# Moving the exponentials' quarters per head group, with ScalarE copying the own quarters, in a two-layer graph kernel with a hand-written order

## The chip, the core and the metric

The kernel runs on one core of a Trainium2 chip. The metric is device time in microseconds (us) of one execution. TensorE (PE in the profile, its weight loads PEld), VectorE (DVE), ScalarE (ACT) and GpSimd (POOL) compute; SyncE (SP) issues nearly all DMAs, and its queue is SPq in the profile.

## The reference

Two layers over 128 graphs of 128 nodes with 256 features, all in float32. Cut to what matters:

```python
# layer 0: attention with an adjacency mask, then an FFN
q, k = heads(src @ Wq + bq), heads(src @ Wk + bk)          # 8 heads of 32
attn = softmax(q k^T / sqrt(32), axis=-1)                  # over all nodes
out = sum over r in 0..3 of (attn * (adj == r)) @ heads(src @ Wv[r] + bv[r])
x = ln(src + out @ Wo + bo); x = ln(x + gelu(x @ W1 + b1) @ W2 + b2)
# layer 1: two graph attentions, then an FFN
for W, a in (W1, a1), (W2, a2):
    Wh = h @ W
    e = leaky_relu(Wh @ a[:256] + (Wh @ a[256:])^T, 0.2)
    h = softmax(where(adj > 0, e, -9e15), axis=1) @ Wh
x = ln(x + h); x = ln(x + relu(x @ w_ff1 + b) @ w_ff2 + b)
```

The adjacency holds only 0 and 1. The softmax's sums in layer 0 run over all nodes, so they need the exponentials before the mask.

## The kernel before

The 16384 rows are worked in 32 groups (NG) of 512 rows: 4 graphs. A group has two pairs p of graphs. For each group there are generators, one for each kind of work, which issue a few instructions per step: `in` and `rest` load; `bo` prepares the residual; `q` makes q, k and v (tiles pqqa, pqqb, pvqa, pvqb on TensorE; `projected`, from group 2 on with seven products in place of eight); `a` is attention; `d` gathers the softmax's sums; `n0` to `n3` are the layer norms, which also copy x into 16-bit planes (L464) and transpose them by DMA into pT (L467); `t0` to `t2` copy pT into yT (L492); `f` and `fc` are two halves of the first FFN, `l` the two graph attentions (pw L1093, py, pg on TensorE), `k` and `kc` the second FFN, `out` the store.

The order in which all these steps are issued is written by hand in three strings, FRONT, STEADY and TAIL. A token is a step and the group it is for, relative to the current one; `a:1*3` takes three steps of the next group's attention. STEADY is run for groups 1 to 29. Nothing reorders it: each engine runs its instructions in the order of these tokens, and waits on semaphores where data or a buffer isn't ready.

The FFNs multiply with seven products of half-size blocks. `others` works in the banks ph1/po1 (tag fa) and ph7/po7 (tag fe), `chain` in the one bank seeded: ScalarE copies the first product into seeded (L620, L647, L649), TensorE adds products to it, ScalarE copies it out (p16 L628, and p7 L583 from ph7), VectorE forms hT's quarters (L591 from ph7, L632 from seeded) and their sums h2, h3 (L640 to L644). A product that reuses seeded waits for its last reader.

In attention, `scores` makes four tiles ps, one for each head group s (L858), and one exponential for each (L865) into e, a tile of 128 partitions with the keys along the partitions: `e[:, s]` is 512 numbers for each key. `masked` multiplies by the adjacency into pm (L875); `sums` multiplies e and pm with v into pav (L970). e, pm and es have one buffer each.

The softmax's sums are taken on VectorE from group 2 on (`turned_sums`). Key quarters (32 partitions each) and head groups must be exchanged so that four quarters of a head group lie on the same partitions. For that SP moves 32-partition blocks of e into four parts: es[:, 0], es[:, 1], and ea's two; for p=0 ea lies in the upper half of pm, for p=1 in the tag wh. Then VectorE adds the four (L901, L903, L905), transposes and reduces. Part k of head group s comes from quarter (s + k) mod 4, so that part 0 is a copy within the same partitions. pm's upper half is masked only when the sums over it are folded.

Of the kernel before, what the change touches and what calls it, by code (L numbers as in the profile page):

```python
# [120 lines left out]


FRONT = """
in:0 Lqk*4 Lgat q:0 Lv Lo q:0*2 wqk q:0 rest:0 q:0 L1 Lv*3 q:0*3 a:0 Lv_ a:0 Lv_ q:0 a:0*2 in:1
Lv_ d:0 a:0*2 d:0*2 q:0 a:0 d:0*4 q:0 a:0 L3 d:0 a:0 q:0 L1 q:0 L1 q:0 a:0 Lh1 a:0*6 Lh1 a:0 L2
L1 a:0*2 d:0 a:0 q:1 L1 d:0 Lg1 a:0*2 L4 d:0 q:1*2 q:0 w1 d:0*3 a:0 rest:0 q:1 w1 q:1 d:0 q:1*2
d:0 q:0 a:0 q:1 a:0*2 a:1*3 Lg1 bo:0*2 L1 a:0*2 wqk Lgat rest:1 a:1*2 Lg1 a:1 a:0*2 L2 d:1*2 a:0
L2 d:1 L4 Lg1 a:1 a:0 L3 a:0*4 d:1 bo:0 b1 q:1 d:1 n0:0 d:1 a:1 d:1 rest:1 q:1 n0:0 b1 q:1 d:1
n0:0 q:1*2 output_bias n0:0 a:1 n0:0 w1 n0:0 output_bias Lh1 q:1 b1 wv a:1*2 w1 a:1 gw n0:0 t0:0
a:1*2 t0:0 a:1 f:0 t0:0*2 a:1 b1 a:1*2 L3 d:1 t0:0 fc:0 a:1 b1 t0:0 a:1 d:1 L2 q:1 a:1 d:1*2 Lgat  # L130
Lg2 f:0 q:1 fc:0 wqk Lgat fc:0 b1 f:0 L4 a:1 d:1 Lg2 a:1 b1 fc:0 d:1 f:0 L3 d:1 Lh1 d:1 b1 f:0
a:1 f:0 a:1 w2 Lh2 fc:0 f:0 fc:0 a:1 fc:0 w2 f:0 fc:0 gw fc:0 L4 gw f:0 a:1*2 fc:0 wv a:1*2
bo:1*2 fc:0 wv in:2 L3 fc:0 L3 f:0 fc:0*2 f:0 wqk a:1 f:0 a:1 fc:0 f:0 fc:0 f:0*2 a:1*2 fc:0*2 w2
f:0 c1 fc:0*3 rest:2 fc:0 a:1*2 f:0 fc:0 w2 f:0 n0:1 c1 fc:0 n0:1*2 fc:0 n0:1*2 f:0*2 fc:0 q:2
f:0*2 n0:1 bo:1 fc:0*3 n0:1 f:0 q:2 fc:0 f:0 t0:1 fc:0 t0:1 fc:0 gw n1:0*2 q:2 t0:1*2 gw gelu
n1:0 q:2 n1:0 q:2 n1:0 c1 q:2 f:1 q:2 n1:0 t0:1 c1 q:2*2 n1:0 q:2 t1:0 c1 t1:0 f:1 q:2 l:0 fc:1
t0:1 f:1 t1:0 l:0 u1 l:0 t1:0 fc:1 l:0*4 f:1 fc:1 l:0 fc:1 f:1 Lh2 q:2 l:0 f:1 fc:1 q:2*2 fc:1*2
f:1 fc:1 f:1 fc:1 q:2 fc:1 q:2*2 f:1 fc:1 q:2 u2 l:0 c1 l:0*2 f:1 c1 fc:1 l:0 a:2 l:0*2 f:1 a:2
f:1 l:0 a:2 fc:1 l:0*2 a:2 exp l:0*2 q:2 a:2 u2 l:0*4 fc:1 wv l:0*3 q:2 u2 fc:1*2 q:2 d:2 l:0
fc:1 d:2 f:1 l:0 fc:1 q:2 u1 fc:1 u1 f:1*2 d:2 f:1 q:2 u1 d:2 q:2 d:2 q:2 l:0 a:2*2 fc:1 l:0*2  # L140
f:1 fc:1 q:2 d:2 q:2 fc:1 l:0 c1 l:0*2 f:1 q:2 f:1 l:0*2 fc:1 l:0*2 fc:1 l:0*2 u2 d:2 l:0 fc:1
l:0*2 f:1 fc:1 l:0*2 n2:0 f:1 d:2 n2:0*6 t2:0 fc:1 t2:0 fc:1 q:2 t2:0 fc:1 a:2*2 rest:2
"""
STEADY = """
q:1 f:0 q:1*2 f:0 t2:-1 fc:0 a:1*4 k:-1 fc:0 d:1 f:0 a:1*2 t2:-1 d:1 kc:-1 t2:-1 a:1*3 k:-1*2
fc:0 d:1 kc:-1 a:1 kc:-1 a:1 k:-1 a:1 k:-1 a:1*3 d:1*2 n1:0 k:-1 kc:-1 d:1 k:-1 kc:-1 k:-1 n1:0
k:-1 kc:-1 n1:0 a:1 kc:-1 n1:0*2 a:1 kc:-1 bo:1 n1:0 d:1 a:1 k:-1 kc:-1 d:1*3 a:1*5 kc:-1*4 k:-1
n1:0 in:2 kc:-1 t1:0*2 k:-1*2 t1:0 k:-1 kc:-1 t1:0 k:-1 l:0*2 k:-1 kc:-1 k:-1 bo:1 l:0*2 kc:-1
bo:1 a:1*2 kc:-1 l:0 kc:-1 a:1 l:0 kc:-1 l:0 a:1 l:0*2 k:-1 n0:1 kc:-1*2 n0:1 kc:-1 k:-1 kc:-1
k:-1 n0:1 kc:-1 n0:1*2 k:-1 kc:-1*2 n0:1 rest:2 n0:1 l:0*2 kc:-1 l:0*2 kc:-1 k:-1 l:0 q:2 t0:1  # L150
q:2 t0:1 q:2 l:0*2 k:-1 t0:1 kc:-1 l:0 f:1 l:0*2 t0:1 kc:-1 q:2*2 fc:1 q:2 t0:1 q:2 f:1*2 l:0
t0:1 q:2 gelu f:1 l:0*3 k:-1 l:0 fc:1 q:2 kc:-1 l:0 fc:1 l:0 fc:1*2 l:0 f:1*2 q:2 l:0 fc:1*2 l:0
f:1 fc:1 f:1 fc:1 n3:-1 f:1 fc:1*2 f:1 fc:1 q:2 fc:1 f:1 q:2 n3:-1 f:1*3 fc:1 l:0 q:2 fc:1 l:0
f:1 q:2 fc:1 q:2 l:0 n3:-1 q:2 f:1 l:0 q:2 fc:1*2 q:2 f:1 fc:1 l:0*2 fc:1 a:2 fc:1 f:1 fc:1 a:2
l:0 a:2 l:0*4 f:1 a:2 q:2 a:2 fc:1 a:2 l:0 a:2 l:0*2 q:2 l:0 q:2 l:0 d:2*2 fc:1 f:1 q:2*2 l:0
d:2*2 q:2 d:2 q:2 n2:0 d:2 out:-1 fc:1 n2:0 f:1 n2:0 fc:1 n2:0*4 q:2 t2:0*3 d:2 fc:1 q:2 fc:1 q:2
fc:1 q:2 d:2 a:2 exp rest:2 a:2
"""
TAIL = """
q:1 f:0 t2:-1 q:1*2 d:1 fc:0*2 a:1 t2:-1 f:0 a:1*3 f:0 a:1 fc:0 k:-1 a:1 k:-1 kc:-1 a:1 k:-1*2  # L160
d:1 k:-1 a:1 t2:-1 d:1 kc:-1 k:-1 n1:0 a:1 kc:-1 n1:0 kc:-1 k:-1 a:1 kc:-1 d:1 n1:0 d:1 k:-1 a:1
n1:0 kc:-1 k:-1 n1:0 a:1*3 kc:-1 a:1 bo:1 kc:-1*3 k:-1 kc:-1 d:1 kc:-1 k:-1 d:1 n1:0 k:-1 kc:-1
a:1 k:-1 n1:0 t1:0 d:1 t1:0 kc:-1 a:1*2 l:0 d:1*2 kc:-1 l:0 t1:0 a:1 kc:-1 l:0 bo:1 t1:0 k:-1 a:1
l:0*5 a:1 k:-1 a:1 l:0 a:1*4 k:-1 kc:-1 a:1 k:-1 kc:-1 bo:1 kc:-1*2 k:-1 n0:1 kc:-1*2 n0:1
kc:-1*2 k:-1 kc:-1 l:0*3 k:-1 kc:-1 l:0 n0:1 l:0 n0:1 l:0 n0:1*3 t0:1 l:0*2 t0:1 l:0*2 k:-1*2 l:0
kc:-1 l:0 kc:-1*2 l:0*2 kc:-1*2 t0:1 l:0*3 k:-1 t0:1 kc:-1 l:0*2 t0:1 f:1 fc:1 l:0 f:1 l:0*4 t0:1
f:1 fc:1 l:0 fc:1 l:0*2 f:1 l:0 f:1 fc:1*2 f:1 fc:1 f:1 fc:1 l:0*2 f:1*3 l:0 fc:1*2 l:0 fc:1*4
k:-1 f:1 fc:1 f:1 fc:1 l:0*2 f:1 fc:1 f:1*2 l:0 f:1 fc:1*2 l:0*2 fc:1 n2:0 f:1 fc:1 gelu n3:-1
fc:1*2 f:1 fc:1 n2:0 fc:1 n2:0 f:1 n2:0 fc:1 n2:0 f:1 fc:1 n3:-1 fc:1 n2:0 fc:1 f:1 n2:0 t2:0 f:1
fc:1 f:1*2 exp fc:1*2 t2:0 k:0 fc:1 t2:0 n1:1 t2:0 kc:0 t2:0 n1:1*2 t2:0 k:0 kc:0 n1:1 k:0*2 n1:1  # L170
kc:0 n1:1*2 k:0 kc:0*2 t1:1*2 kc:0 n3:-1 k:0*2 kc:0 out:-1 l:1*3 t1:1*2 l:1*3 k:0 l:1*2 kc:0*2
l:1*3 kc:0*2 l:1 k:0 l:1 kc:0 l:1*3 k:0 l:1 k:0 l:1 k:0 l:1 kc:0 k:0*2 kc:0 l:1*5 k:0 l:1*9 k:0
kc:0*2 l:1*2 kc:0*3 k:0 kc:0 l:1*5 kc:0*2 l:1*6 kc:0*2 n2:1 kc:0 k:0 n2:1*4 kc:0 k:0 kc:0 k:0*2
n2:1*2 kc:0 t2:1 k:0 t2:1 kc:0 k:0 t2:1 kc:0*2 k:1 t2:1 kc:1 t2:1 k:1 t2:1 kc:1*2 checks k:1*2
kc:1 k:1*2 kc:1 k:1 kc:1 k:1 kc:1*2 k:0 k:1 kc:0 kc:1*4 k:1 kc:1 k:1*2 kc:1 n3:0 k:1*2 kc:1 k:1*2
kc:1 k:1 kc:1*6 n3:0 k:1 kc:1*2 k:1*2 n3:0 kc:1*2 k:1*2 kc:1*3 k:1*2 z:1 kc:1 z:1 kc:1*2 out:0
z:1*2
"""


# [8 lines left out]
def fast_pass(ctx, tc, a, out):  # L189
# [651 lines left out]
    def scores(S, p):  # L841

        assert {(0, 0, p), (0, 1, p)} <= S["have"]
        qT, kT = S["qT"], S["kT"]
# [17 lines left out]
        yield 1 if p == 0 else None
        S["e", p] = e = w1p.tile([P, HC, 2, NCH, P], F32, tag="e", name="e_" + n)
        for s in range(HC):
            nc.scalar.activation(e[:, s], pss[s], AF.Exp, scale=SCALE)  # L865
# [15 lines left out]
    def turned_sums(S):  # L881

        n = str(S["g"])
        for p in range(G // 2):
            e = S["e", p]
            es = w1p.tile([P, 2, T], F32, tag="es", name=f"es_{n}_{p}")
            ea = None
            if p:
                ea = flat(w1p.tile([P, G, NU], F32, tag="wh", name="ea_" + n))
                ea = ea[:, : 2 * T].rearrange("p (k t) -> p k t", k=2)  # L890
            for k in range(4):
                if k == 2 and p == 0:
                    ea = S["pm", p][:, 2:].rearrange("p s u c i -> p s (u c i)")
                part = (es, ea)[k // 2][:, k % 2]
                for s in range(HC):
                    to, fr = (slice(y * DH, (y + 1) * DH) for y in (s, (s + k) % HC))
                    nc.sync.dma_start(part[to], e[fr, s].rearrange("p u c i -> p (u c i)"))  # L897
# [5 lines left out]
            nc.vector.tensor_add(ea[:, 0], ea[:, 0], ea[:, 1])  # L903
# [679 lines left out]
```

## Time and profile before

| | |
|---|---|
| median of 3 runs | 2649.66 us (2648.33 to 2652.46) |
| the profiled execution: time, span | 2651.96 us, 2650.1 us |
| granted TensorE clock, mean | 0.997 |
| PE busy, 20362 matmuls | 2597.7 us, 98% |
| DVE busy, 6041 instructions | 2324.8 us, 88% |
| ACT busy, 3599 instructions | 1715.9 us, 65% |
| queue of SP and ACT (q1): share of 16 DMA engines | 33.2% |
| L897, the moves of e | 960 issues of 64 KB |
| L875, masking | 162.9 us, 256 instructions of 686 ns mean |
| L865, exponentials | 136.4 us, 256 instructions of 603 ns mean |

Busy times of engines lie beside each other; they don't add up to the span. A matmul's end is modelled, so distances between the starts of matmuls tell more than busy time. In a timeline row the columns are the start in us from the span's start, the length in us, the engine, the line, the operation, output and inputs, and in brackets how long the engine stood idle and what ended that.

### The profile page before, as it was taken

What the parts mean: (1) busy time and instruction counts of PE and PEld (TensorE: products, weight loads), DVE (VectorE), ACT (ScalarE), POOL (GpSimd) and SP (SyncE); (2) the same over time, 40 slices, a digit from 0 to 9 for tenths busy, and PEclk for the clock granted to TensorE, in tenths of its full rate; (3) what the DMA queues carried; (4) which work ended last, traced back from release to release, by engine and by line L of the source; (5) the groups of instructions that cost most, each with busy time, mean ns of one, the idle gap of its engine ahead of it and who ended that gap; (6) DMA issues with size and microseconds to landing.
All of it is one profiled execution on the core that took longest, in us unless ns stands there. A gap on an engine that the chain in (4) does not pass through costs nothing.

```text
span 2650.1 us, 54615 instructions
## 1 busy us (share of the span) xinstructions
PE 2597.7 (98%) x20362; PEld 2293.6 (87%) x20362; DVE 2324.8 (88%) x6041; ACT 1715.9 (65%) x3599; POOL 154.2 (6%) x137
## 2 busy tenths in 40 slices
...
DMA packets 328896, 202.11 MB, mean 76 GB/s; under 512 B 234288, under 2 KB 276400, under 8 KB 328624
## 3 DMA queue, kind: packets, MB, share of 16 engines
q1 hardware_dynamic: 327520, 198.16, 33.2%
q8 instruction: 162, 2.65, 0.4%
...
## 4 chain that ended last, share of the span: by engine, by line
PE 68%; DVE 14%; DMA 7%; ACT 6%; SPq 4%; issue 2%; DVEq 0%; POOL 0%; ACTq 0%; POOLq 0%
PE po L533 12%; PE ph L524 12%; PE seeded L524 10%; PE seeded L533 8%; PE pw L1093 4%; PE pqqa L788 4%; SPq L897 3%; PE pav L970 3%; PE pqqb L788 3%; DMA pT<-planes 3%; PE pwo L1016 2%; PE ps L858 2%; PE py L1106 2%; PE pvqa L788 2%; DMA spread<-hbm 1%
## 5 line engine op out<-in xcount | busy, mean ns | idle before, releaser
L492 ACT COPY yT<-pT 128x512 uint16<-128x512 uint16 x384 | 266.7, 763 | 146.0 <-DMA pT<-planes 145.7
L464 ACT COPY planes<-x 128x512 uint16<-128x512 uint16 x384 | 222.8, 619 | 157.7 <-DVE x L444 155.8
L430 POOL TENSOR_TENSOR rs<-rs,mhalf 128x4 f32<-128x4 f32 x129 | 152.0, 1179 | 2441.5 <-DVE rs L429 2423.2
L524 PE MATMUL seeded<-yS,w_L_gnn_w_ff 128*128 128x256 f32 x768 | 204.5, 389 | 10.0 <-ACT seeded L620 7.9
L865 ACT ACTIVATE e<-ps 128x512 f32<-128x512 f32 x256 | 136.4, 603 | 107.0 <-issue 73.8
L524 PE MATMUL seeded<-yS,w_L_gnn_W 128*128 128x256 f32 x768 | 198.0, 380 | 0.3 <-DVE yS L504 0.3
L524 PE MATMUL ph<-yT,w_L_gnn_W 128*128 128x256 f32 x768 | 193.1, 380 | 0.5 <-ACT yT L492 0.4
L524 PE MATMUL ph<-yT,w_L_gnn_w_ff 128*128 128x256 f32 x768 | 191.0, 384 | 1.3 <-ACT seeded L647 0.7
L406 DVE BATCH_NORM_STATS2 st<-x 128x6 f32<-128x256 f32 x512 | 189.3, 412 | 1.5
L533 PE MATMUL po<-w_L_gnn_w_ff,hT 128*128 128x128 f32 x1536 | 189.7, 277 | 0.0
L533 PEld LDWEIGHTS po<-w_L_gnn_w_ff,hT 128*128 128x128 f32 x1536 | 179.5, 192 | 10.7 <-ACT hT L548 10.4
L533 PE MATMUL po<-w_L_gnn_W,hT 128*128 128x128 f32 x1536 | 187.1, 275 | 0.0
L533 PEld LDWEIGHTS po<-w_L_gnn_W,hT 128*128 128x128 f32 x1536 | 184.0, 192 | 3.2
L548 ACT ACTIVATE hT<-hT,c_L_gnn_b_ff 128x256 f32<-128x256 f32 x256 | 113.1, 502 | 112.2 <-DVE hT L591 111.4
L524 PEld LDWEIGHTS seeded<-yS,w_L_gnn_w_ff 128*128 128x128 f32 x768 | 139.5, 190 | 47.9 <-ACT seeded L620 19.5
L875 DVE TENSOR_TENSOR pm<-e,adj 128x512 f32<-128x512 f32 x256 | 162.9, 686 | 4.0 <-ACT e L865 2.9
L805 ACT COPY pv<-pvqa 128x512 f32<-128x512 f32 x60 | 35.2, 587 | 201.7 <-PE pvqa L788 201.5
L524 PEld LDWEIGHTS seeded<-yS,w_L_gnn_W 128*128 128x128 f32 x768 | 144.2, 190 | 23.6 <-ACT p L628 0.7
L524 PEld LDWEIGHTS ph<-yT,w_L_gnn_w_ff 128*128 128x128 f32 x768 | 143.0, 190 | 24.3 <-ACT seeded L647 1.5
L524 PEld LDWEIGHTS ph<-yT,w_L_gnn_W 128*128 128x128 f32 x768 | 143.3, 190 | 19.4 <-ACT yT L492 1.0
L1093 PE MATMUL pw<-wu,yT 128*128 128x260 f32 x512 | 139.6, 398 | 8.6 <-ACT yT L492 7.5
L632 DVE TENSOR_TENSOR hT<-seeded,p 128x512 f32<-128x512 f32 x128 | 88.1, 688 | 62.0 <-PE seeded L524 60.2
...
## 6 DMA issues: line engine op xcount, KB each, us to landing
es<-e SPq DMA_DIRECT2D x480, 64.0 KB, 2.0
...
pm<-e SPq DMA_DIRECT2D x240, 64.0 KB, 2.0
ea<-e SPq DMA_DIRECT2D x240, 64.0 KB, 2.0
...
```

The costliest lines, as they stand in the source:

```text
L406: nc.vector.bn_stats(st[:, b % 2, :], S["x"][:, b, :])
L430: nc.gpsimd.tensor_tensor(rs[:, bs], rs[:, bs], k.mhalf[:, bs], op=ALU.pow)
L464: nc.scalar.copy(planes[:, :, b], words)
L492: nc.scalar.copy(o.rearrange("p (b t h) -> p h b t", b=2, h=2), pT[:, :, :, c, :])
L524: nc.tensor.matmul(bank[:, s * TH : (s + 1) * TH], wa[:, form, 0, f * P : (f + 1) * P], m, start=start and s == 0, stop=True, skip_group_c ...
L533: nc.tensor.matmul(bank[:, s * P : (s + 1) * P], m[:, f, s * P : (s + 1) * P], wb_[:, form, f, :], start=start and s + f == 0, stop=True, ...
L548: nc.scalar.activation(o[:, s], o[:, s] if src is None else src[:, s * TH : (s + 1) * TH], func, bias=ba[:, f : f + 1],)
L632: nc.vector.tensor_add(hidden(1, 1, r), halves(seeded), halves(B["7", r]))
L788: nc.tensor.matmul(bank[:, s * TH : (s + 1) * TH], *ops, start=start and s == 0, stop=True, skip_group_check=True,)
L865: nc.scalar.activation(e[:, s], pss[s], AF.Exp, scale=SCALE)
L875: nc.vector.tensor_mul(pm[:, s], S["e", p][:, s], S["ad"][:, pair(p), None, :].to_broadcast([P, 2, NCH, P]),)
L1093: nc.tensor.matmul(pw[:, :NU], yT[:, c, b * P : (b + 1) * P], wu[:, c, :], start=(c == 0), stop=(c == NCH - 1),)
```

## The change

In `turned_sums`, the loop over parts with the head groups inside becomes a loop over head groups with three moves each (parts 1 to 3), in one step per head group. Part 0, the own quarter, is no longer moved but copied by ScalarE, four copies of 32x512 in two steps. For groups from 2 on, pm of p=0 is allocated behind the first exponential and not the last. FRONT, STEADY and TAIL are replaced whole. The core of the diff:

```diff
 STEADY = """
-q:1 f:0 q:1*2 f:0 t2:-1 fc:0 a:1*4 k:-1 fc:0 d:1 f:0 a:1*2 t2:-1 d:1 kc:-1 t2:-1 a:1*3 k:-1*2
-fc:0 d:1 kc:-1 a:1 kc:-1 a:1 k:-1 a:1 k:-1 a:1*3 d:1*2 n1:0 k:-1 kc:-1 d:1 k:-1 kc:-1 k:-1 n1:0
...
-fc:1 q:2 d:2 a:2 exp rest:2 a:2
+n1:0 k:-1 n1:0 kc:-1 n1:0 d:1*2 a:1 k:-1 kc:-1 d:1 a:1 kc:-1*2 bo:1 a:1 d:1 a:1 kc:-1 a:1*4
+kc:-1*3 n1:0 in:2 kc:-1 n1:0 k:-1 t1:0*2 kc:-1 k:-1*2 t1:0 k:-1 l:0*2 k:-1 kc:-1*2 bo:1 t1:0
...
+k:0 n1:1 kc:0 a:2 k:0 n1:1 k:0
 """
...
         for s in range(HC):
             nc.scalar.activation(e[:, s], pss[s], AF.Exp, scale=SCALE)
-            if s == HC - 1:
+            if s == (0 if S["turned"] and p == 0 else HC - 1):
                 S["pm", p] = w1p.tile([P, HC, 2, NCH, P], F32, tag="pm", name="pm_" + n)
             yield 1 if s == HC - 1 or (p and s == 1 and S["g"]) else None
...
-            for k in range(4):
-                if k == 2 and p == 0:
-                    ea = S["pm", p][:, 2:].rearrange("p s u c i -> p s (u c i)")
-                part = (es, ea)[k // 2][:, k % 2]
-                for s in range(HC):
-                    to, fr = (slice(y * DH, (y + 1) * DH) for y in (s, (s + k) % HC))
-                    nc.sync.dma_start(part[to], e[fr, s].rearrange("p u c i -> p (u c i)"))
-                    if s == 1 and k == 0:
-                        yield
-                yield
+            if p == 0:
+                ea = S["pm", p][:, 2:].rearrange("p s u c i -> p s (u c i)")
+            flat_e = e.rearrange("p s u c i -> p s (u c i)")
+            for s in range(HC):
+                to = slice(s * DH, (s + 1) * DH)
+                for k in range(1, HC):
+                    f = (s + k) % HC * DH
+                    nc.sync.dma_start((es, ea)[k // 2][to, k % 2], flat_e[f : f + DH, s])
+                yield
+            for s in range(HC):
+                own = slice(s * DH, (s + 1) * DH)
+                nc.scalar.copy(es[own, 0], flat_e[own, s])
+                if s % 2:
+                    yield
             nc.vector.tensor_add(es[:, 0], es[:, 0], es[:, 1])
             yield
```

What the new STEADY does on TensorE, beside what stays: the second FFN's first product ph1 comes before pav of p=0, where it came behind ps of p=1; behind ps come ph7, seeded, ph1, ph7, seeded, ph1, pav of p=1, ph7, seeded (before: ph1, ph7, seeded, ph1, ph7, seeded, ph1, pav, seeded, ph7); pw's first product comes ahead of a seeded product, not behind it; po7 of the first FFN comes ahead of the fourth pvqb. On VectorE, L632 of the second FFN's first round comes behind four passes of the layer norm (L444), where it followed L591. On ScalarE, the third and fourth exponential of p=1 come behind the copies of p7 and p16, and behind an activation of hT; behind the fourth come the four copies of own quarters.

More of the change, by code (lines that the diff above doesn't have):

```diff
@@ L123 @@
 FRONT = """
[L124 to L141, printed above, removed]
@@ L142 @@
-l:0*2 f:1 fc:1 l:0*2 n2:0 f:1 d:2 n2:0*6 t2:0 fc:1 t2:0 fc:1 q:2 t2:0 fc:1 a:2*2 rest:2
+Lqk in:0 Lqk q:0 Lqk Lv q:0 L1 q:0 Lv q:0 Lqk L1 in:1 Lv q:0 Lv_ q:0*2 Lv q:0 rest:0 Lv_ a:0*3 L1
+q:0 d:0 a:0 Lv_ a:0 d:0 a:0*2 d:0 L1*2 d:0 q:0 d:0*2 Lh1 d:0 a:0 d:0 a:0 q:0*2 rest:1 q:0*2
+rest:0 wqk a:0*7 q:1 L2 w1 a:0 L4 a:0*3 q:1*2 d:0 bo:0 d:0 Lgat Lg1 a:0*2 d:0*2 q:1 L2 Lg1 d:0 w1
+d:0 q:1 bo:0 q:1 q:0 d:0 Lo q:1 d:0 q:0 q:1 bo:0 a:0*4 L1 a:1 a:0*2 a:1 a:0 rest:1 wqk w1 a:0
+a:1*2 a:0 a:1 L3 a:1 Lg1 d:1 a:0 d:1 Lg1 d:1 a:1 a:0*2 q:1 a:0*2 Lg2 d:1 Lgat n0:0 b1 d:1*2 L2
@@ new lines @@
+a:1 d:1 n0:0 q:1 b1 q:1 n0:0 L4 q:1 wqk d:1 q:1 Lgat n0:0 a:1 b1 output_bias n0:0 wv L2 q:1
+n0:0*2 t0:0 b1 a:1 output_bias t0:0 a:1 Lh1*2 a:1*3 Lgat a:1*2 gw f:0 a:1 t0:0 a:1 b1 L3 a:1 b1
+w2 a:1 t0:0 w1 t0:0*2 d:1 fc:0 b1 gw q:1 Lg2 d:1*3 a:1 f:0 fc:0 f:0 b1 f:0 a:1 fc:0*3 d:1 L4 d:1
+f:0 q:1 fc:0 f:0 fc:0 f:0 d:1 f:0 Lh2 gw L3 a:1 f:0 d:1 a:1 f:0*2 a:1 fc:0 a:1 fc:0*2 bo:1 w2
+bo:1 fc:0*2 a:1*3 f:0 a:1 wqk fc:0 in:2 fc:0 gw a:1 L3 f:0 a:1 fc:0 f:0 fc:0*2 a:1 f:0 w2 a:1 Lh1
+bo:1 a:1 L3 a:1 f:0 fc:0*3 f:0 wv n0:1 L3 fc:0 q:2 f:0 fc:0 c1 fc:0 f:0 n0:1 q:2 fc:0 w2 n0:1
@@ new lines @@
+fc:0 q:2 n0:1 t0:1 n0:1 f:0 c1 t0:1 fc:0 f:0 L4 fc:0 c1 n0:1 fc:0 wv fc:0 f:0*2 n0:1 q:2 fc:0 q:2
+f:0 fc:0*2 q:2 n1:0*2 gw n1:0 Lh2 n1:0 q:2 t0:1 n1:0*2 c1 n1:0 q:2 t0:1 c1 u1 f:1 q:2*3 t0:1 c1
+f:1 t1:0*2 c1 l:0 gelu u2 fc:1 t1:0 l:0 t0:1 t1:0 l:0*2 fc:1 f:1 l:0 fc:1 l:0*2 fc:1 l:0 q:2 l:0
+f:1*3 fc:1*3 f:1*3 fc:1 rest:2 fc:1*2 q:2*2 exp q:2 fc:1 l:0*2 u1 l:0 q:2 u1 q:2 f:1 q:2 l:0 fc:1
+f:1 l:0 a:2 l:0 u2 l:0 fc:1 l:0*3 a:2 f:1 fc:1*2 a:2 l:0 fc:1 l:0 a:2*2 l:0*3 a:2 l:0*2 u2 u1 d:2
+l:0 d:2 l:0 fc:1 f:1 l:0 f:1 wv f:1*2 fc:1*2 l:0 d:2 fc:1 l:0 d:2 f:1 a:2 l:0 u2 q:2 l:0 fc:1 c1
@@ L143 @@
+l:0*2 fc:1 q:2 l:0*2 f:1 l:0*2 d:2*2 l:0 q:2 fc:1 q:2*2 l:0 f:1 d:2 q:2 l:0*2 q:2 l:0*2 q:2 l:0
+n2:0 q:2*2 d:2 n2:0 fc:1*2 q:2 f:1 n2:0*2 d:2 fc:1 n2:0*2 a:2 fc:1 f:1 n2:0 fc:1 q:2 t2:0 f:1
+rest:2 t2:0 q:2 fc:1 t2:0*2 fc:1 k:0 a:2 q:2 a:2*3 d:2 fc:1 f:1 kc:0 a:2 d:2 t2:0 a:2 k:0 f:1 a:2
+k:0 a:2 k:0 a:2 t2:0 fc:1 a:2 d:2*2 kc:0 a:2 kc:0 a:2 d:2 a:2 k:0 a:2 k:0 d:2 n1:1 a:2 d:2 a:2
+k:0 n1:1 k:0 kc:0
 """
 STEADY = """
-q:1 f:0 q:1*2 f:0 t2:-1 fc:0 a:1*4 k:-1 fc:0 d:1 f:0 a:1*2 t2:-1 d:1 kc:-1 t2:-1 a:1*3 k:-1*2
@@ L146 @@
-fc:0 d:1 kc:-1 a:1 kc:-1 a:1 k:-1 a:1 k:-1 a:1*3 d:1*2 n1:0 k:-1 kc:-1 d:1 k:-1 kc:-1 k:-1 n1:0
[L147 to L156, printed above, removed]
-fc:1 q:2 d:2 a:2 exp rest:2 a:2
+n1:0 k:-1 n1:0 kc:-1 n1:0 d:1*2 a:1 k:-1 kc:-1 d:1 a:1 kc:-1*2 bo:1 a:1 d:1 a:1 kc:-1 a:1*4
@@ new lines @@
+kc:-1*3 n1:0 in:2 kc:-1 n1:0 k:-1 t1:0*2 kc:-1 k:-1*2 t1:0 k:-1 l:0*2 k:-1 kc:-1*2 bo:1 t1:0
+k:-1*2 l:0*2 kc:-1 a:1*2 kc:-1 l:0 kc:-1 l:0 a:1 kc:-1 l:0 kc:-1*2 l:0*2 kc:-1 k:-1 a:1 n0:1
+kc:-1 k:-1 n0:1*2 kc:-1 k:-1 n0:1 bo:1 n0:1 q:2 k:-1 kc:-1 n0:1*2 kc:-1 l:0 kc:-1 l:0 k:-1
+kc:-1*2 q:2 l:0 q:2 l:0*2 t0:1*2 q:2 kc:-1 l:0 rest:2 f:1 k:-1 l:0 t0:1*2 q:2*2 l:0*2 fc:1 q:2
+gelu l:0 t0:1 l:0 f:1*3 t0:1 l:0*2 fc:1 l:0 f:1 l:0*3 k:-1 q:2 f:1 fc:1 l:0 kc:-1 l:0 f:1 fc:1
+f:1*2 q:2 n3:-1 l:0 fc:1*3 q:2 fc:1 f:1 fc:1*3 q:2 fc:1*2 f:1 q:2 f:1 q:2 n3:-1 fc:1*2 f:1*2 q:2
```

39 lines of the change are left out of this document (21 added, 18 removed).

## The prediction

> **What bounds the kernel now.** I read the page first (which engine is full), then busy time by stretches (where it is not), the list of waits (who holds TensorE up), and the timeline of one group (what each wait hangs on).
>
> ```profile
> span 2650.1 us, 54615 instructions
> PE 2597.7 (98%) x20362; PEld 2293.6 (87%) x20362; DVE 2324.8 (88%) x6041; ACT 1715.9 (65%) x3599; POOL 154.2 (6%) x137
> ```
>
> TensorE is the bound, VectorE is next, ScalarE has room. The profiled execution took 2651.96 us, 2.3 above the median of 2649.66; I subtract from the median what I find in the 2650.1 us span.
>
> ```profile
> 0.00:160.00 160.00, 149.66 (x1200) 120.79 (x1200) 115.87 (x310) 90.14 (x177) 7.04 (x12) 0.98 0.44 114
> 960.00:1120.00 160.00, 158.96 (x1261) 141.17 (x1259) 143.37 (x373) 106.38 (x224) 9.44 (x8) 1.00 0.32 75
> 2560.00:2650.00 90.00, 73.90 (x487) 64.19 (x486) 64.34 (x184) 42.88 (x93) 7.46 (x7) 0.96 0.17 37
> ```
>
> Columns after the length: PE, PEld, DVE, ACT and POOL busy, granted clock (full), DMA share, GB/s. Start and end hold 10.3 + 16.1 us of the 52.4 us in which PE is not busy; the 2400 us between hold 26, so 0.9 per group of 81 us.
>
> That count is too small, because a matmul's end is modelled. Back to back, four 128x256 matmuls start 0.86 us after the last four; a larger distance between starts is a stall, even inside "busy". Here the Trainium skill ("Perfetto Trace Analysis", Identifying the Most-Contended Engine) says matmul busy share is a bad measure and weight-load busy share a good one. By it, 13% of 2650 us, some 345 us, would be free. The rows speak against that: weight loads lie beside matmuls that stand at their 0.86 us distance nearly everywhere, so most of the 13% is no room. I count late starts.
>
> ```profile
> PEld pw L1093 <- ACT yT L492: 26.6, 54, 1.2
> PEld seeded L524 <- ACT seeded L620: 20.2, 30, 0.9
> PEld po L533 <- ACT hT L548: 10.4, 26, 0.4
> PEld pav L970 <- DVE v L803: 10.1, 30, 0.7
> PEld pvqb L788 <- DVE pv L803: 6.2, 11, 0.9
> DVE ea L903 <- DMA ea<-e: 25.6, 23, 1.7
> ```
>
> Total us, times, longest. The first five are TensorE's repeated waits: 73.5 us, 2.5 per each of the 29 passes of STEADY. The weight loads run about 0.2 us ahead of their matmuls, so some 1.0 of that is not lost: 1.5. In the group around 890 us the starts give
>
> ```profile
> 887.99 1.03 PE L524 MATMUL ph<-yS,w_L_gnn_w_ff 128*128 128x256 f32 x4
> 889.40 0.62 ACT L865 ACTIVATE e<-ps 128x512 f32<-128x512 f32 x1
> 889.56 1.13 PE L524 MATMUL seeded<-yS,w_L_gnn_w_ff 128*128 128x256 f32 x4 [0.54 <-ACT seeded L620]
> 893.18 5.78 SPq L897 DMA_DIRECT2D ea<-e  x8
> 893.78 0.68 DVE L632 TENSOR_TENSOR hT<-seeded,p 128x512 f32<-128x512 f32 x1
> 895.96 1.13 PE L524 MATMUL seeded<-yS,w_L_gnn_w_ff 128*128 128x256 f32 x4
> 899.06 2.64 SPq L467 DMA_TRANSPOSE pT<-planes  x2
> 902.36 1.40 ACT L492 COPY yT<-pT 128x512 uint16<-128x512 uint16 x2 [1.14 <-DMA pT<-planes]
> 903.18 1.33 PE L1093 MATMUL pw<-wu,yT 128*128 128x260 f32 x4
> 904.50 2.05 PE L533 MATMUL po<-w_L_gnn_w_ff,hT 128*128 128x128 f32 x16
> ```
>
> seeded 1.57 after ph instead of 0.86: 0.71 lost. pw to po 1.32 instead of 0.88: 0.44; pw itself 0.22 late. With pvqb (1.30 from 876.63 to 877.93, 0.44) and pav (0.26 on L803) it is 2.07. Read off in the same way over 22 passes, the means are 0.45 at seeded, 0.61 at pw, 0.25 at po, 0.2 at pvqb and 0.2 at pav: 1.7 per pass, between the two counts. Note SP: planes of the first pair were copied by 896.8, but their transpose issues at 899.06, right after the last of the moves.
>
> **The change, part by part.** *Moves.* Each e loses 4 of 16 moves: 240 of 960.
>
> ```profile
> L897 SPq DMA_DIRECT2D es<-e x480: 507/584/2059, 121.2 to 2511.2; - x160
> es<-e SPq DMA_DIRECT2D x480, 64.0 KB, 2.0
> ```
>
> An issue holds SP 0.584 us, landing takes 2.0. The Trainium skill ("DMA: Bandwidth & Descriptors", Issuing engines are not separate DMA queues) calls the sequencer's time to start a DMA usually small relative to the DMA: by that, dropping four would be worth nothing on the path. Here 16 issues took 888.06 to 898.96, 10.9 us, five times the landing, and everything later on SP stands behind them. I take the row: 4 x 0.68 = 2.7 us less per e, with 2.3 (4 x 0.584) as the other end. The three moves of a head group follow its own exponential, so none waits for another group's. At p=1 SP is free about 9 us after the scores end, not 12 (887.02 to 899.06). The transposes then wait for ScalarE's planes, not SP: about 9.0 and 11.9 against 12.0 and 13.4, so yT comes 1.5 to 3 us earlier. L903's 25.6 us of waiting goes too.
>
> *Own quarters.* 240 copies of 32x512 on ScalarE. Nearest row:
>
> ```profile
> L939 ACT COPY pm<-e 64x512 f32<-64x512 f32 x16 | 9.9, 616 | 0.2
> ```
>
> 148 us in all, ScalarE to 70%; back to back it can be 0.5 each (exponentials: three in 1.58). Four cost 2.0 to 2.5. At p=0 they fit in the 6.4 us in which ScalarE waits for pvqa before 874.19: nothing. At p=1 behind them stand the activation of hT's second quarter and planes_1; that activation needs L591's sum on VectorE, 6.4 after the scores, and the copies end at 6.9: 0.5 late, and its reader h3 comes 8 us later on VectorE: nothing on TensorE. Without that cover it costs 0.5 per pass.
>
> *pm allocated at the first exponential.* It lets pm be masked and filled earlier; no instruction added.
>
> *Order of the steady pass.* Which steps move past which, from the new instruction order (lines numbered as in the kernel before):
> - ph1 (first product of the second FFN) now stands before pav of p=0, so the copy L620 has pav, ps and ph7 (3.9 us) to cover it: the 0.45 mean (0.71 shown) goes. pav comes 0.86 later and waits no more for v (0.26).
> - po7 (1.78) moves ahead of the pvqb that waited for L803: its 0.2 mean goes (0.44 shown).
> - pw moves ahead of one seeded product, 0.86 earlier, while yT is 1.5 to 3 us earlier: from 0.61 to about 0.15. po's wait for hT (0.25) goes, as the activation no longer queues behind late yT copies.
> Gone: 0.45 + 0.2 + 0.2 + 0.46 + 0.25 = 1.56; with smaller ones (yS into ph, pw on pwo's bank) 1.7.
> - New: L632, the sum that frees seeded, is put behind four affine passes (0.4 each, two pairs in 1.7 us). TensorE had 1.5 us in hand there (894.46 to 895.96) and gets ph7 in between (+0.86), but arrives 1.3 earlier by the stalls removed: 1.06 in hand against 1.7. VectorE gains up to 0.8 by not waiting for the moves. So 0 to 0.65; I take 0.25.
> - New: in the first FFN the table load (1.28) and its dummy stand before the copy of p7, and p16's copy behind two yh. p16 is then ready about 0.25 after TensorE asks; bounds 0 and 0.5, I take 0.2.
> - Exponentials 3 and 4 of p=1 now stand behind p7, p16 and an hT pair. From the end of the scores: exponentials at 0.4 and 0.9, p7 1.4, p16 2.15 (after seeded), third 2.65, hT 3.2, fourth 4.0 to 4.6, mask 5.4 to 5.8; pav, six products later at 5.3 to 5.4, asks for the last mask at 5.75. About 0.1.
> VectorE has the same work; it runs without a gap from 857 to 900 us, so only small delays can be caught up there.
>
> *FRONT and TAIL.* Loads, first groups and last products are reordered too. PE's 26 us of idle there is partly first loads and last result. No row prices the new order: at most 6 won, 6 lost, I take 0.
>
> Sum: 1.7 - 0.25 - 0.2 - 0.1 = 1.15 per pass, times 29 = 33 us: 2649.7 - 33 = 2616.7, so 2617.
>
> **The rivals.** *VectorE takes most of it back.* Between 857 and 900 us VectorE has no gap, so a stall removed before pav may return at the next mask. Then only the pw and po part stays, 0.71, less 0.45 of new waits: 0.3 per pass, 2641 (2632 to 2650). For it: VectorE at 143 of 160 us. Against: TensorE's waits there name late inputs by 0.2 to 0.7, and VectorE loses its own waits for moves.
>
> *Slower: the last exponential is late.* If ScalarE runs each piece at its lone duration (0.6, 0.85 a pair) with a semaphore's delay between, the fourth ends beyond 6, the mask at 7.2; pav waits 1.4, L591, the affine passes and L632 shift as much, and seeded waits 0.65 and more behind it: with p16, 2.3 lost against 1.7 won, 0.6 x 29 = +17, 2667 (2655 to 2680). It decides from about 1.7 us of new waits per pass, which means a fourth exponential ending later than about 6.2 after the scores. Against it: ScalarE copies start 0.5 apart in the trace when queued.
>
> *Everything goes.* New waits are nil, and the small ones vanish: 2.0 per pass, 58 us, with 4 at the ends: 2588 (2580 to 2604).
>
> **How the numbers follow.** About 0.2% (5.3 us) is what a measurement of this kernel can tell from no change. Forecast 0.60 (2604 to 2632), VectorE takes it back 0.20 (mostly faster by over 0.2%, a third within it), slower 0.13, everything 0.07. Faster 0.60 + 0.07 + 0.13 = 0.80; within 0.06; slower 0.14 (0.13, and 0.01 of the second case). The range leaves out the deepest part of the last case and the upper part of the slow one: 2598 to 2658.
>
> **What would show it.** Right: the distance from ps to ps of p=1 falls from 81.1 to about 79.9; seeded's wait on the L620 copy is gone; the transposes of planes_1 issue about 9 us after the scores' end; L903's wait for ea is near 0; SP's 16 issues are 12. Wrong: pav or seeded waiting on pm or hT by over 0.5 per pass, hT activations waiting behind es copies with TensorE behind them, or gains and losses at start and end of over 6 us.

## The result, and the profile after

| | before | after |
|---|---|---|
| median | 2649.54 us (2648.33 to 2652.46) | 2609.48 us (2608.4 to 2611.15) |
| ratio, 95% interval | | 0.9848 (0.9831 to 0.9865) |
| span of the profiled execution | 2650.1 us | 2609.4 us |
| us from the scores of p=1 of one group to those of the next, mean of 28 passes | 80.95 | 79.41 |

The change saves 40 us. The 28 passes between the scores of groups 2 and 30 take 43.3 us less. What comes ahead of them is 0.3 longer, what comes behind them 2.3, so FRONT and TAIL gave nothing.

The engines' busy times, after:

```profile
PE 2566.4 (98%) x20362; PEld 2286.5 (88%) x20362; DVE 2329.3 (89%) x6041; ACT 1883.0 (72%) x3841; POOL 142.1 (5%) x137
```

The same matmuls are done in a shorter span, VectorE's work is unchanged, and ScalarE has 167 us more. In the busy time by stretches (the columns as in the prediction) the middle hardly moves:

```profile
960.00:1120.00 160.00, 159.51 (x1270) 142.51 (x1269) 145.91 (x377) 118.77 (x243) 8.67 (x8) 1.00 0.31 71
```

PE's busy time there rose by 0.55 of 160 us, 0.3%, where a pass became 1.9% shorter: busy time again counts stalls as work. The list of waits says which stalls went (total us, times, longest):

```profile
PEld seeded L525 <- ACT seeded L648: 15.9, 60, 0.6
PEld pg L1124 <- ACT e L866: 10.8, 29, 0.4
PEld seeded L525 <- DVE hT L633: 10.5, 42, 1.5
PEld pw L1098 <- ACT yT L493: 4.1, 12, 1.0
PEld po L534 <- ACT hT L549: 2.1, 1, 2.1
DVE ea L908: 4.9, 10
```

(The last line is from the view of the moves' line, who waited for it.) pw's wait for yT went from 26.6 to 4.1, po's for hT from 10.4 to one time at the start. The waits of seeded on L621, of pvqb on v and of pav on v no longer stand among the large ones. VectorE's wait for ea fell from 25.6 to 4.9. New is pg's wait on the exponentials, and L648 and L633 now hold seeded.

The line of the moves, and that of the copies (count, then total and mean ns):

```profile
L899 SPq DMA_DIRECT2D es<-e x240: 513/535/1678, 120.5 to 2468.8; - x120
L903 ACT COPY es<-e 32x512 f32<-32x512 f32 x240 | 147.1, 613 | 4.5
```

720 moves are left of 960. A copy takes 613 ns, and four in a row 2.53 us. One pass in the timeline, from the scores of p=1 on:

```profile
951.27 0.57 ACT L621 COPY seeded<-ph 128x512 f32<-128x512 f32 x1 [4.83 <-DVE x L667]
951.36 1.17 PE L859 MATMUL ps<-qT,kT 32*128 32x128 f32 x32
956.24 0.62 ACT L866 ACTIVATE e<-ps 128x512 f32<-128x512 f32 x1
956.72 2.53 ACT L903 COPY es<-e 32x512 f32<-32x512 f32 x4
959.27 0.91 ACT L549 ACTIVATE hT<-hT,c_L_gnn_b_ff 128x256 f32<-128x256 f32 x2
959.49 2.16 SPq L899 DMA_DIRECT2D ea<-e  x2
960.09 1.12 ACT L465 COPY planes<-x 128x512 uint16<-128x512 uint16 x2
961.11 0.91 ACT L549 ACTIVATE hT<-hT,c_L_gnn_b_ff 128x256 f32<-128x256 f32 x2
961.93 0.81 ACT L549 ACTIVATE hT<-seeded,c_L_gnn_b_ff 128x256 f32<-128x256 f32 x2
962.08 1.34 SPq L468 DMA_TRANSPOSE pT<-planes  x1
962.77 0.57 ACT L648 COPY seeded<-ph 128x512 f32<-128x512 f32 x1
963.39 1.13 PE L525 MATMUL seeded<-yS,w_L_gnn_w_ff 128*128 128x256 f32 x4
```

Two things are to be seen. ScalarE has no gap from the copies to L648, behind which TensorE starts seeded 0.05 us after the copy has ended: the copies fit, with nothing to spare. And in this pass the moves end at 961.65, late because the last two took 2.16 us, and the transpose follows at 962.08. In 16 of 29 passes SP is done earlier, and the first transpose starts 0.03 us behind the copy of the planes, as in the next pass, where the moves end at 1040.18:

```profile
1039.55 1.12 ACT L465 COPY planes<-x 128x512 uint16<-128x512 uint16 x2
1040.70 1.44 SPq L468 DMA_TRANSPOSE pT<-planes  x1
```

Late starts of TensorE (distance between the starts of two matmuls less the distance that they keep in a row), the mean per pass over 22 passes, show what went and what came:

| in us per pass | before | after |
|---|---|---|
| pav (on v, and changes of shape) | 0.75 | 0.04 |
| pw (yT, bank) | 0.81 | 0.34 |
| seeded behind L620 / L621 | 0.54 | 0 |
| po on hT | 0.23 | 0 |
| ph on yS | 0.23 | 0 |
| pvqb on v | 0.19 | 0 |
| pg on exponentials 3 and 4 | 0.01 | 0.45 |
| seeded on L633 (its place in the new order) | 0 | 0.18 |
| seeded, another product of the same FFN (before: it follows pav of p=1, change of shape) | 0.28 | 0.03 |
| ph behind pav of p=1 (the same change of shape, new order) | 0 | 0.28 |
| all late starts | 4.15 | 2.55 |

The difference, 1.60, is near the 1.54 that a pass gained. More than half of the 2.55 is the same in every pass (changes of tile shape, 0.13 to 0.28 each). One of these has only moved: from pav of p=1 to the first matmul of the next product it is 1.88 us in both kernels, that product being seeded before and ph after.

### The profile page after: what moved, and what is told of

Read it like the earlier page. It is cut to its first block, busy times and chain, and to the rows that moved or that the text cites. A ratio compares the mean times of both kernels' runs of the same rounds, so it can differ in the third digit from the quotient of the medians.

```text
span 2609.4 us, 54584 instructions
## 1 busy us (share of the span) xinstructions
PE 2566.4 (98%) x20362; PEld 2286.5 (88%) x20362; DVE 2329.3 (89%) x6041; ACT 1883.0 (72%) x3841; POOL 142.1 (5%) x137
## 4 chain that ended last, share of the span: by engine, by line
PE 83%; ACT 7%; DVE 5%; DMA 3%; issue 1%; SPq 1%; POOL 0%; DVEq 0%; ACTq 0%; POOLq 0%
PE ph L525 14%; PE po L534 14%; PE seeded L534 12%; PE seeded L525 11%; PE pqqa L789 4%; PE pvqa L789 4%; PE pav L975 4%; PE pw L1098 4%; PE pqqb L789 3%; PE pvqb L789 3%; PE pwo L1021 3%; ACT e L866 3%; PE ps L859 3%; PE pg L1124 2%; PE py L1111 2%; ACT hT L549 1%
## 5 line engine op out<-in xcount | busy, mean ns | idle before, releaser
L431 POOL TENSOR_TENSOR rs<-rs,mhalf 128x4 f32<-128x4 f32 x129 | 140.0, 1085 | 2406.7 <-DVE rs L430 1893.4
L876 DVE TENSOR_TENSOR pm<-e,adj 128x512 f32<-128x512 f32 x256 | 169.2, 682 | 0.4 <-ACT e L866 0.2
L903 ACT COPY es<-e 32x512 f32<-32x512 f32 x240 | 147.1, 613 | 4.5
L621 ACT COPY seeded<-ph 128x512 f32<-128x512 f32 x64 | 37.4, 584 | 135.9 <-DVE x L667 135.2
L1098 PE MATMUL pw<-wu,yT 128*128 128x260 f32 x512 | 133.2, 389 | 2.3 <-ACT wh L1103 1.3
```

The costliest lines, as they stand in the source:

```text
L431: nc.gpsimd.tensor_tensor(rs[:, bs], rs[:, bs], k.mhalf[:, bs], op=ALU.pow)
L876: nc.vector.tensor_mul(pm[:, s], S["e", p][:, s], S["ad"][:, pair(p), None, :].to_broadcast([P, 2, NCH, P]),)
L903: nc.scalar.copy(es[own, 0], flat_e[own, s])
L1098: nc.tensor.matmul(pw[:, :NU], yT[:, c, b * P : (b + 1) * P], wu[:, c, :], start=(c == 0), stop=(c == NCH - 1),)
```

## The experiments

Each kernel was timed in five rounds against the kernel before on the same chip; where a figure in us is compared across two runs, it is the difference to before. Line numbers differ by a few between the kernels.

| kernel | ratio to before (95%) | us against before |
|---|---|---|
| after | 0.9848 (0.9831 to 0.9865) | -40.1 |
| x1: new order, 16 moves, no copies | 1.0142 (1.0127 to 1.0158) | +37.1 |
| x2: old order, new moves and copies | 1.0262 (1.0248 to 1.0276) | +70.2 |
| x8: the same, copies early | 1.0116 (1.0101 to 1.0132) | +31.8 |
| x11: old order, new moves, no copies | 0.9966 (0.9955 to 0.9977) | -9.0 |
| x12: new order, new moves, no copies | 0.9852 (0.9837 to 0.9867) | -40.3 |
| x6: after, copies twice | 1.0184 (1.0170 to 1.0198) | +49.6 |
| x7: after, one add less on VectorE | 0.9844 (0.9830 to 0.9857) | -40.6 |
| x4: after, ph1 behind ps, copy late | 1.0000 (0.9992 to 1.0008) | +1.3 |
| x10: after, ph1 behind ps, copy early | 0.9843 (0.9829 to 0.9856) | -41.8 |
| x5: after, L633 first | 0.9872 (0.9857 to 0.9887) | -32.1 |
| x3: after, pg behind pvqa | 0.9814 (0.9801 to 0.9828) | -49.7 |
| x9: x3, copies of p=1 on GpSimd | 0.9888 (0.9873 to 0.9903) | -29.7 |

**x1, the new order without the freed SP.**

```diff
-                for k in range(1, HC):
+                for k in range(HC):
                     f = (s + k) % HC * DH
                     nc.sync.dma_start((es, ea)[k // 2][to, k % 2], flat_e[f : f + DH, s])
...
-                nc.scalar.copy(es[own, 0], flat_e[own, s])
```

> The new order with 16 moves per e on SP, in head-group order (the own quarter is moved too, as part 0 of its head group), and no ScalarE copies. Theory (the freed time on SP lets the new order work): the second pair's transposes issue some 2 us later than in the changed kernel (about 11.5 us behind the scores instead of 9.6), yT is late, and pw, which the new order asks for earlier, waits 0.8 to 1 us more per pass: +25 us, near 2635. Rival (the order alone gives the gain, the moves are hidden): within 5 us of the changed kernel's 2609. Rival (ScalarE's copies cost time): faster than 2604.

77 us slower than after, and slower than before: the new order needs the freed SP, and by three times the expected amount. Its waits, and the timeline of one pass behind scores that start at 980.42:

```profile
PEld pw L1096 <- ACT yT L493: 69.4, 62, 2.8
992.19 1.22 SPq L899 DMA_DIRECT2D ea<-e  x2
993.51 1.26 SPq L468 DMA_TRANSPOSE pT<-planes  x1
996.63 1.38 ACT L493 COPY yT<-pT 128x512 uint16<-128x512 uint16 x2 [1.86 <-DMA pT<-planes]
997.44 1.33 PE L1096 MATMUL pw<-wu,yT 128*128 128x260 f32 x4 [1.30 <-ACT yT L493]
```

The planes were copied by 990.74; the transpose waits for the last of the 16 moves at 993.41. In the median the first transpose comes 11.8 us after the scores' end, the second 13.9; with 12 moves it is 8.8 and 11.9. pw, which the new order asks for earlier, waits 65 us more in all; the rest of the 77 is in smaller waits behind it (pav on pm 8.0 against 0.8, pw on wh 6.1, L633 15.0 against 10.5).

**x2 and x8, the moves and copies in the old order.** The changed `turned_sums` with the steps of before:

```diff
+            for s in range(HC):
+                for k in range(1, HC):
+                    nc.sync.dma_start((es, ea)[k // 2][to, k % 2], flat_e[f : f + DH, s])
+                if s:
+                    yield            # x8: only if s == 1
+            for s in range(HC):
+                nc.scalar.copy(es[own, 0], flat_e[own, s])
+                if s % 2:
+                    yield            # x8: one step behind all four, three empty steps
```

> The order of before with the new moves (12 per e, by head group) and the ScalarE copies in the steps where parts 2 and 3 were moved. Theory (moves and order each take a part): the wait of pw and po for late yT goes (0.6 to 0.85 per pass), the wait of seeded on its own copy, of pav on v and of pvqb stays: -17 to -24 us, near 2629. Rival (the moves are the gain): 2609 to 2615. Rival (the order is the gain): within 5 us of 2649.5.

> The order of before with the new moves, as in x2, but with all four ScalarE copies straight behind the last exponential's step. In x2 the copies stood behind the copy of a pvqa, ScalarE waited for TensorE there, and VectorE's add of es, with the sum behind it that frees seeded, waited 4.1 us for them: 119 us in 29 passes. Theory (only the copies' place made x2 slow; by themselves the moves take away the wait for late yT): the wait of the add goes, and the time is 2625 to 2640. Rival (the moves per head group don't fit the old order wherever the copies stand): over 2660.

x2 is 70 us slower than before; neither its theory nor a rival had that. At p=0:

```profile
972.09 0.58 ACT L805 COPY pv<-pvqa 128x512 f32<-128x512 f32 x1 [5.29 <-PE pvqa L788]
972.70 1.25 ACT L903 COPY es<-e 32x512 f32<-32x512 f32 x2
973.98 0.69 DVE L906 TENSOR_TENSOR es<-es 128x512 f32<-128x512 f32 x1 [4.10 <-ACT es L903]
974.59 0.42 DVE L654 TENSOR_TENSOR x<-seeded,x 128x256 f32<-128x256 f32 x1
975.07 3.68 PE L533 MATMUL seeded<-w_L_gnn_W,hT 128*128 128x128 f32 x16 [2.15 <-DVE x L654]
```

ScalarE waits for a product before it does two copies, VectorE waits in its add for the copies, the sum behind the add frees seeded, and TensorE waits for that: 73.9 us in 29 passes. x8 takes this away, but is still 32 us slower than before: the rival's number. Its reason is only part of it, as x11 will show. At p=1 the copies now stand ahead of p16's copy:

```profile
979.61 2.53 ACT L903 COPY es<-e 32x512 f32<-32x512 f32 x4
982.16 0.59 ACT L628 COPY p<-seeded 128x512 f32<-128x512 f32 x1
982.80 1.13 PE L524 MATMUL seeded<-yS,w_L_gnn_w_ff 128*128 128x256 f32 x4 [1.13 <-ACT p L628]
```

L628 now holds seeded up for 48.1 us in all. In the new order the third and fourth exponential, and the copies with them, come behind p7 and p16. No run puts the copies behind p16 in the old order. Such a place has a gap in the kernel before:

```profile
893.90 1.72 ACT L548 ACTIVATE hT<-hT,c_L_gnn_b_ff 128x256 f32<-128x256 f32 x4 [1.47 <-DVE hT L591]
```

So x2 and x8 price the old order with the copies where these two runs have them; that a better place exists there is neither shown nor ruled out.

**x11 and x12, the copies left out in both orders.**

```diff
-                nc.scalar.copy(es[own, 0], flat_e[own, s])
...
-            nc.vector.tensor_add(es[:, 0], es[:, 0], es[:, 1])
+            nc.vector.tensor_add(es[:, 0], es[:, 1], es[:, 1])
```

> x8 (order of before, 12 moves by head group) with the ScalarE copies left out: the sums lack the own quarter, whose place in the first add is taken by part 1 again, so that VectorE's work stays the same. Theory (two costs made x8 slow: the copies in ScalarE's row ahead of p16's copy L628, 1.6 us of wait at seeded per pass, and the add of es at p=0, which in the old order stands too early for moves that all land late, 1.0 at pvqb): the first goes, the second stays, and the waits of pw and po for late yT are gone: 0.990 to 1.000 of before. Rival (the copies were not it, the moves' order alone upsets the old order): 1.006 or more. The prediction's sum for the moves, without any cover used up, would be 0.990.

> The changed kernel with its ScalarE copies left out in the same way (own quarter missing in the sums, same work on VectorE, 12 moves). Theory (in the new order the copies just fit: what TensorE waits for behind them comes at most 0.05 to 0.3 late): 0 to -8 us against the changed kernel, 0.982 to 0.985 of before. Rival (ScalarE's row at p=1 is the bound of the changed kernel and each us of it costs TensorE a us, as the second set of copies did): -1 us per pass or more, 0.974 or less.

Both came out as the theory had them, x12 at the upper end. In the old order, where x8 has them, the copies cost 41 us (x8 against x11), in the new order nothing that can be measured (after against x12). Why, x12's row of ScalarE behind the fourth exponential shows:

```profile
956.74 0.91 ACT L549 ACTIVATE hT<-hT,c_L_gnn_b_ff 128x256 f32<-128x256 f32 x2 [1.57 <-DVE hT L592]
960.11 0.84 ACT L549 ACTIVATE hT<-seeded,c_L_gnn_b_ff 128x256 f32<-128x256 f32 x2 [0.24 <-PE seeded L525]
```

Without copies ScalarE stands idle there for 2.1 us in the median, with them for 0.1, and L648 starts 10.1 and 10.2 us behind the scores' end. The copies fill a wait that is there anyway. Without them the old order has lost its wait for yT and kept, in x11's waits,

```profile
PEld pvqb L788 <- DVE pv L803: 27.6, 29, 1.6
PEld seeded L524 <- ACT seeded L620: 19.8, 30, 0.7
DVE es L906 <- DMA es<-e: 31.6, 29, 2.1
```

The add of es waits for the moves, since by head group all parts land late, where before the parts of es came first; L803 stands behind it, and pvqb waits. Together with x1 and x8 this makes a table of ratios:

| | 16 moves | 12 moves, copies | 12 moves, own quarter left out |
|---|---|---|---|
| old order | 1 (before) | 1.0116 | 0.9966 |
| new order | 1.0142 | 0.9848 | 0.9852 |

As tried here, neither half of the change makes the kernel faster. For the moves' half this hangs on where x2 and x8 put the copies: with the copies left out it gains 9 us (x11). (The 16 moves of before go by part, those of x1 by head group; 12 moves by part were not tried, nor pm's earlier allocation by itself.)

**x6, the copies twice.**

```diff
-                nc.scalar.copy(es[own, 0], flat_e[own, s])
+                for _ in range(2):
+                    nc.scalar.copy(es[own, 0], flat_e[own, s])
```

> The changed kernel with each ScalarE copy of an own quarter done twice: 240 copies more, 2.5 us more of ScalarE per e (147 us in all). Theory (the copies lie in ScalarE's waits and cost nothing): within 5 us of the changed kernel, whose ratio to before is 0.985. Rival (four copies fill the gap at p=1, and what is queued behind them, the activation of hT's second quarter and the planes, is already on the path): +1 us per pass or more, 2640 or over.

The rival holds, at 90 us against after:

```profile
PEld seeded L525 <- ACT seeded L648: 88.3, 60, 2.9
983.62 5.08 ACT L904 COPY es<-e 32x512 f32<-32x512 f32 x8
992.22 0.57 ACT L648 COPY seeded<-ph 128x512 f32<-128x512 f32 x1
992.85 1.13 PE L525 MATMUL seeded<-yS,w_L_gnn_w_ff 128*128 128x256 f32 x4 [2.46 <-ACT seeded L648]
```

The second set takes 2.55 us at p=1, and the wait of seeded on L648 is 72.4 us larger: 2.5 per pass. The shortest passes, a time that several passes share in each run, take 81.54 us against 78.98 in after. ScalarE has no slack there at all beyond the four copies. (Some of the remaining 17 us are passes at a lower clock, see the last section.)

**x7, less work for VectorE.** `- nc.vector.tensor_add(ea[:, 0], ea[:, 0], ea[:, 1])`

> The changed kernel without the second of the three adds of the softmax's sums (L908, 0.69 us of VectorE, two per pass): the sums leave out one of four quarters, so that 1.4 us of VectorE work are left out per pass, 40 us in all. Theory (TensorE sets the pace; VectorE's work is covered but for a few late inputs): -3 to -10 us. Rival (VectorE sets the pace): -25 to -40 us.

40 us of VectorE's work left out move the time by 0.5 us against after. VectorE, busy 89% of the span, doesn't set the pace: its shortest passes take 78.97 us against 78.98. The intervals, some 4 us to each side, can't tell the 3 us that the theory expected from none.

**x4 and x10, ph1 behind the scores again.** In x4 the copy L621 (L620 in these runs) stands behind p7 and the third exponential, in x10 behind the second and ahead of p7:

```diff
-k:0 f:1 exp a:2 fc:1 kc:0 d:2 a:2*2 rest:2 a:2 k:0 kc:0 d:2 a:2 k:0*2 kc:0 a:2 k:0
+f:1 exp a:2 fc:1 d:2 a:2*2 rest:2 a:2 k:0*2 d:2 a:2 k:0 a:2 kc:0*2 k:0 kc:0 k:0      # x4
+f:1 exp a:2 fc:1 d:2 a:2*2 rest:2 a:2 k:0 a:2 kc:0 k:0 kc:0 d:2 k:0*2 kc:0 a:2 k:0   # x10
```

> The changed kernel with ph1 of the second FFN put behind the scores of p=1 again, and the copy L621 behind the third exponential, as before; STEADY alone. Theory (ph1's place is what removed the wait of seeded on that copy): seeded waits 0.45 to 0.7 again and pav of p=0 comes 0.86 earlier and waits 0.1 to 0.2: +13 to +25 us, near 2627. Rival (the earlier ph1 is worth little because VectorE's masks come next): under +5 us.

> The changed kernel with ph1 behind the scores of p=1 as in x4, but with its copy L621 straight behind the first two exponentials, ahead of p7 (in x4 it stood behind the third, where it made seeded wait 2.1 us). Theory (what ph1's early place is worth is that L621's 0.57 us lie ahead of ScalarE's full stretch and not in it): L648 and the products behind it come 0.6 later, seeded behind L621 some 0.1 to 0.3: 0.6 to 0.9 per pass, +17 to +25 us against the changed kernel (0.985), so 0.991 to 0.994. Rival (the place doesn't matter once the copy is early): within 0.002 of 0.985.

x4 loses 41 us against after, more than was expected:

```profile
966.19 0.59 ACT L583 COPY p<-ph 128x512 f32<-128x512 f32 x1 [0.81 <-PE ph L524]
966.67 0.60 ACT L865 ACTIVATE e<-ps 128x512 f32<-128x512 f32 x1
967.16 0.60 ACT L620 COPY seeded<-ph 128x512 f32<-128x512 f32 x1
967.82 1.13 PE L524 MATMUL seeded<-yS,w_L_gnn_w_ff 128*128 128x256 f32 x4 [1.67 <-ACT seeded L620]
```

But x10 equals after (-41.8 against -40.1 us, intervals overlap), so the theory that L621 must lie ahead of ScalarE's full stretch falls as well. seeded waits for the copy by no more than 0.2 at a time (5.8 us in all). TensorE has ph1, ph7, seeded in a row in x10 as before, and seeded comes 0.86 behind ph7, which is its distance without a wait. What made the old wait was the copy's place on ScalarE, behind the third exponential; that ph1 stands earlier on TensorE is worth nothing that can be measured.

**x5, L633 ahead of the affine passes.** One `kc:-1` is taken from near the head of STEADY and TAIL and put at the ends of FRONT and STEADY, where `k:0 n1:1 k:0` becomes `k:0 kc:0 n1:1 k:0` in STEADY.

> The changed kernel with the sum L633 of the second FFN's first round straight behind L592 again, ahead of the last three affine passes (L445), in FRONT, STEADY and TAIL. Theory (L633's place costs the new order what the prediction said: 0.25 per pass, 0.18 by the late starts in the changed kernel): -5 to -7 us, near 2603. Rival (the affine passes come 0.7 later, so planes, transposes and yT do, and pw waits that much longer): +5 to +20 us.

The rival holds, at its lower end: nothing is gained, and 8 us are lost if the two intervals, which just overlap, are taken at their centres. L633's wait falls from 10.5 to 4.0 us in all, L648's rises from 15.9 to 20.7, since the planes' copy stands ahead of L648 on ScalarE and now comes later. The two sums trade places; L633's late start can't be had back by moving it.

**x3, pg behind pvqa.** `l:0 d:2 q:2` becomes `d:2 q:2 l:0` in STEADY.

> The changed kernel with pg of the first pair (L1124) put one product later, behind pvqa, in STEADY alone. In the changed kernel this pg starts 0.45 us late per pass, since its bank is that of the exponentials 3 and 4 of p=0. Theory (a late start of TensorE there is lost time): pvqa's 0.95 us cover it, and 28 x 0.45 = 13 us go: 2597. Rival (VectorE sets the pace and takes it back at the next mask): within 3 us of 2609.

The best kernel of all: 0.9814, 0.0034 or 9.6 us below after. pg's wait is gone from the list, but TensorE, earlier by 0.45, then waits 0.28 at seeded on L633 (15.2 us in all against 10.5). So the shortest passes gain only 0.13: 78.85 us against 78.98, some 4 us in all. The rest of the 9.6 lies in passes that take longer than that (the mean is 79.06 here, 79.41 in after); why those lose less in x3 is not shown.

**x9, GpSimd copies the own quarters of p=1.** `(nc.gpsimd.tensor_copy if p else nc.scalar.copy)`, the last two behind GpSimd's pow.

> x3 (the changed kernel with pg behind pvqa) with the four copies of p=1 on GpSimd in place of ScalarE (those of p=0 stay); the last two behind GpSimd's pow of the layer norm. x6 showed that ScalarE has no slack behind these copies at p=1: L648, which TensorE waits for, stands in the same unbroken row. Theory: 2.5 us of that row go, what is left of seeded's wait on L648 goes (0.28 per pass in x3), and pw's few late yT too: -4 to -10 us against x3's 0.981 of before, so 0.977 to 0.980. Rival (GpSimd is slow for 32x512, its pow or the add of es on VectorE waits for it): above 0.985.

The rival holds, by a mechanism that it did not name. ScalarE's row does get gaps, but beside GpSimd's copies VectorE's affine passes slow down, and L633 stands behind them:

```profile
959.23 1.69 POOL L903 COPY es<-e 32x512 f32<-32x512 f32 x2
959.62 1.58 DVE L444 SCALAR_TENSOR_TENSOR x<-x,rs,r_L_gnn_beta 128x256 f32<-128x256 f32 x2
961.12 0.68 DVE L632 TENSOR_TENSOR hT<-seeded,p 128x512 f32<-128x512 f32 x1
961.85 1.13 PE L524 MATMUL seeded<-yS,w_L_gnn_w_ff 128*128 128x256 f32 x4 [0.71 <-DVE hT L632]
```

Two passes take 1.58 us; in x3 they take 0.88. seeded's wait on L632 is 35.3 us in all against 15.2 in x3: the 20 us that x9 loses.

## Why the prediction was right, and where it was not

The total (2617 against 2609.5, in the likeliest case's range) and its main chain hold; a pass gained 1.54 us where 1.15 was said. Several terms are wrong in size, and two of the reasons are wrong.

- **SP's relief: right.** Said: 2.7 us less per e, the transposes 9.0 and 11.9 us behind the scores' end, waiting for the planes and no longer for SP. Measured, in the median: the first from 11.8 to 8.8, the second from 13.2 to 11.9. The second always waits for the planes, the first in 16 of 29 passes. The Trainium skill ("DMA: Bandwidth & Descriptors", Issuing engines are not separate DMA queues) would have this at about nothing; x1 prices it at 77 us in the new order, so the row decides. VectorE's wait for ea fell to 4.9 us, not quite to 0.
- **The waits gone: undersized.** Said 1.7 per pass. By the late starts it is about 2.4: pav 0.71 in place of 0.2, ph on yS 0.23 among "smaller ones", the rest within 0.1 of the terms. For pav only the wait on v that the rows name was counted. From pav's first matmul at p=0 to the first of the scores it is 2.60 us before and 1.88 after.
- **The new waits: wrong ones.** Said 0.55 (L632, now L633: 0.25; p16: 0.2; last exponential: 0.1). L633 shows 0.18, p16 and the last exponential hardly anything. Missed altogether was pg of the first pair, 0.45 per pass: the new order puts it ahead of pvqa, and its bank is that of exponentials 3 and 4. It is a step that neither the prediction nor the section on the change lists as moved. That 0.18 and 0.45 come near the 0.55 is luck.
- **"seeded's 0.45 goes because ph1 stands ahead of pav": wrong reason.** The wait went, but x10 has ph1 behind ps and the same time.
- **"The copies cost nothing": right in the sum, half right in the cover.** The wait for L591's sum, which the prediction named, is most of what the copies fill (1.57 of 2.1 us in x12). What comes behind was not seen: the prediction had 8 us in hand up to h3, but L648 stands in the same ScalarE row, and it has no slack. x6 shows 2.5 us of TensorE for 2.5 of ScalarE. Four copies take 2.53 us, the upper end of what was said.
- **Parts were added up as if each stood alone.** The table shows +37 and +32 us for each half as tried and -40 for both. The expectation of x2, made for one half with the same terms, has the wrong sign.
- **VectorE as the next bound: refuted** by x7. The stretch from 857 to 900 us, read as without a gap, holds gaps of 0.37 and 0.78 us. The rival "the last exponential is late" did not come about either: the fourth exponential ends at 956.86, 4.3 us behind the end of the scores at 952.5, within the 4.0 to 4.6 that was said.
- **FRONT and TAIL at 0, within 6:** 2.5 us longer were measured.

What stays open: the waits on v that the rows name at pav are about half of the 0.71; why the matmuls behind them came later still, no run shows.
